# Rows of h by VectorE block turns and transfers over DRAM in place of TensorE transposes

## The chip, the cores and the metric

The kernel runs on one core of one Trainium2 chip. The metric is the device time of one execution in microseconds (us), taken as the median of several runs. The engines are TensorE (PE, its weight loads are listed as PEld), VectorE (DVE), ScalarE (ACT), GpSimd (POOL) and the queue engine SyncE (SP), which here only issues transfers.

## The reference

The inputs are x (16 batches x 1024 nodes x 128 features, fp32), one 1024 x 1024 matrix adj used by all batches, and small weights. Layer 0 is a graph convolution with a residual and a layer norm, layer 1 is a gated recurrent update that runs five steps on the same adj:

```python
x = layernorm(x + adj @ (x @ W0) + b0)
h = x
for _ in range(5):
    m  = adj @ h                                   # for every batch; used twice (m_in = m_out)
    av = concat([m, m])
    u3 = h @ u3_w.T + u3_b
    z  = sigmoid(av @ w3_w.T + w3_b + u3)
    r  = sigmoid(av @ w4_w.T + w4_b + u3)
    hv = tanh(av @ w5_w.T + w5_b + (r * h) @ u5_w.T + u5_b)
    h  = (1 - z) * h + z * hv
out = layernorm(x + h)
```

All arithmetic is fp32.

## The kernel before

**Tiling.** The batches go through in four quads of four (`QUAD`). `adj` is transposed once and kept in SBUF. The product adj times four batches, `aggregate` (L340), is done with a two-level Strassen-like scheme: seven outer products instead of eight, each again seven inner ones. It runs as four chains of matmuls (`chain`, L296) named by their outer products: chain 12 (products 1 and 2), chain 3, chain 67 and chain 54. A chain runs its inner products in a fixed order, 1, 5, 6, 2, 7, 3, 4, with hooks: work that is hung in front of an inner product. In a chain the stationary operand of a matmul is a 128 x 128 block of h (or of sums of blocks), the moving operand 256 columns of adj or of its sums. One fp32 matmul is two matmul instructions of the profile. Chains 12, 67 and 54 have 28 matmuls each, chain 3 has 14.

**Two layouts of h.** `rows` holds h with nodes on the partitions: `rows[p, k, c, d]` is node 8p + c of batch k, feature d, so that `rows[:, k, c, :]` is a stationary block for chunk c. `hid` holds h with features on the partitions, for the gates. DVE forms the outer sums of blocks into `tsum` (`outer_sums`, L286) and the inner ones into `inner` (`sums_of`, L282, `inner_sums`, L265).

**A recurrent step.** The program loops over quads q and steps s (L536). After `aggregate` has left m in `agg` (features on the partitions), for each batch k `gate_half` (L396) runs three matmuls per half of the nodes, and `update` (L420) two, a tanh on ACT and three operations on DVE that leave the new h in `hid` (L430 to L432). The next step's aggregation needs the new h in `rows`: `back_to_rows` (L441) transposes each of the eight chunks of a batch on PE into PSUM (`turn`, L434, L438), and ACT copies them to `rows` (L444), 512 columns at a time. In steps 1 to 4 batches 0 and 1 are turned between the gates, batches 2 and 3 in hooks 6 and 7 of chain 12. Then come the sums: the inner sums of batches 0 and 1 (L267 to L270) are wanted by product 5 of chain 12, the rows and sums of batches 2 and 3 by chain 3, the outer sums (L290 to L294) by chains 67 and 54. In step 0 of a quad it is the other way round: `rows` comes from DRAM and `to_hidden` (L446) makes `hid` by transposes, hung into chains 3 and 67.

**Order.** The tile framework orders the instructions of each engine by priority and by its own estimate of times, and puts in the semaphores; after that each engine runs its list in order. Transfers of the recurrent part are issued by SP. PSUM banks for gates and transposes come from a pool of three (`bank`, L88).

Of the kernel before, what the change touches and what calls it, by code (L numbers as in the profile page):

```python
# [20 lines left out]
def kernel(  # L21
# [29 lines left out]

    nc = tc.nc
# [4 lines left out]
    QT = N // 4  # L57
    CH = C // 2
# [11 lines left out]
    rows = const.tile([P, QUAD, C, D], F32, name="rows")  # L70
    hid = const.tile([P, QUAD, N], F32, name="hid")
    agg = const.tile([P, QUAD, N], F32, name="agg")
    tsum = const.tile([P, 4, 2, CH, D], F32, name="tsum")
    first = const.tile([P, 2, N], F32, name="first")
    hvs = const.tile([P, 2, HALF], F32, name="hvs")
    inner = [const.tile([P, 4, 2, 2, D], F32, name=f"inner{i}") for i in range(2)]
    ypad = [const.tile([P, C, D], F32, name=f"ypad{i}") for i in range(2)]

    z_of = [tsum[:, i].rearrange("p k c d -> p (k c d)") for i in (1, 0)]
    rh_of = [tsum[:, i].rearrange("p k c d -> p (k c d)") for i in (2, 3)]  # L80
    hid_rows = hid.rearrange("p b (c d) -> p b c d", c=C)
    saved = dram.tile([B, P, N], F32, name="saved")

# [9 lines left out]

    def load(q, dst, src_of, ks=range(QUAD)):
        for k in ks:
            nc.sync.dma_start(dst[:, k], src_of(q * QUAD + k))

    def x_rows(b):
        return as_rows(b, x)

    def saved_rows(b):
        return saved[b].rearrange("p (c d) -> p c d", c=C)
# [3 lines left out]
    adj_rows = adj.rearrange("(p c) m -> c p m", c=C)  # L106
    raws = [agg[:, c] if c < CH else hid[:, c - CH] for c in range(C)]
    for h in range(2):
        for c in range(h * CH, h * CH + CH):
            queues[c % 2].dma_start(raws[c], adj_rows[c])  # L110
        for k in (2 * h, 2 * h + 1):
            queues[k % 2].dma_start(rows[:, k], x_rows(k))
# [159 lines left out]
    def blocks_of(src, ns):  # L272

        halves = src.rearrange("p b (h j c) d -> p b h j c d", h=2, j=2)
        if ns == (1, 2):
            return lambda j, k: halves[:, k, :, j]
        if ns == (3,):
            return lambda j, k: halves[:, 2 + k, 1:2, j]
        at = {(6, 7): slice(1, 3), (5, 4): slice(0, 4, 3)}[ns]
        return lambda j, k: tsum[:, at, k, 2 * j : 2 * j + 2]  # L280

    def sums_of(src, ns):  # L282
        t = inner[0 if ns in ((1, 2), (6, 7)) else 1]
        inner_sums(blocks_of(src, ns), [t[:, i, : len(ns)] for i in range(4)])

    def outer_sums(src, early=True, late=True):  # L286

        lo, hi = src[:, 0:2], src[:, 2:4]
        if early:
            nc.vector.tensor_sub(tsum[:, 2], hi[:, :, CH:], hi[:, :, :CH])  # L290
            nc.vector.tensor_add(tsum[:, 1], tsum[:, 2], lo[:, :, :CH])
        if late:
            nc.vector.tensor_sub(tsum[:, 0], hi[:, :, :CH], lo[:, :, :CH])
            nc.vector.tensor_sub(tsum[:, 3], lo[:, :, CH:], tsum[:, 1])  # L294

    def chain(tag, src, ns, results, hooks, order=(1, 5, 6, 2, 7, 3, 4)):  # L296


        xs = blocks_of(src, ns)
        t = inner[0 if ns in ((1, 2), (6, 7)) else 1]  # L300
        w = len(ns) * QT
        right = {
            1: xs(0, 0), 2: xs(1, 0), 3: xs(1, 1), 4: t[:, 3], 5: t[:, 0], 6: t[:, 1], 7: t[:, 2],
        }
# [19 lines left out]
        for a in order:  # L324
            for hook in hooks.get(a, ()):
                hook()
            for o, n in enumerate(ns):
                for c in range(2):
                    nc.tensor.matmul(  # L329
                        bank_of[a][:, ts(o, QT)], right[a][:, o, c, :], left[n][a][:, c, :],  # L330
# [9 lines left out]
    def aggregate(tag, src, hooks):  # L340

        c12 = agg[:, 2:4, :HALF]
        room = src.rearrange("p b c d -> p b (c d)")
# [5 lines left out]
        def into(t):  # L349
# [3 lines left out]
        chain(f"12_{tag}", src, (1, 2), into(first), hooks.get(12, {}))  # L353
        sums_of(src, (6, 7))
        nc.vector.tensor_add(agg[:, 0:2, :HALF], two(first[:, 0]), two(first[:, 1]))
        chain(
            f"3_{tag}", src, (3,), lambda i, k: agg[:, 2 + k : 3 + k, ts(i, QT)], hooks.get(3, {}),
        )
        sums_of(src, (5, 4))
        p6, p7, p5, p4 = (room[:, k] for k in range(4))  # L360
        chain(f"67_{tag}", src, (6, 7), into(room[:, 0:2]), hooks.get(67, {}))
# [4 lines left out]
            f"54_{tag}", src, (5, 4), into(room[:, 2:4]), hooks.get(54, {}),  # L366
# [9 lines left out]
    def project(q, k, y):  # L376

        b = q * QUAD + k
        for h in range(2):
# [6 lines left out]
            for c in range(CH):  # L386
                nc.tensor.matmul(  # L387
                    po3[:, c, :], agg[:, k, ts(h * CH + c, P)], w0_sb, start=False, stop=True,
                    skip_group_check=True,
                )  # L390
            with tc.high_priority():
                nc.vector.tensor_add(y[:, ts(h, CH), :], po3, y[:, ts(h, CH), :])
        layernorm(y, f"0_{b}", saved_rows(b))
# [26 lines left out]
    def update(tag, k):  # L420

        z, rh = z_of[k % 2], rh_of[k % 2]
        for h in range(2):
# [8 lines left out]
            nc.vector.tensor_add(hid[:, k, cols], hid[:, k, cols], hv)  # L432

    def turn(name, src):  # L434
        pt = bank(name)
        pt3 = pt.rearrange("p (k q) -> p k q", k=CH)
        for c in range(CH):
            nc.tensor.transpose(pt3[:, c, :], src(c), ident)  # L438
        return pt3

    def back_to_rows(tag, k):  # L441
        for h in range(2):
            pt = turn(f"pt_{tag}_{k}_{h}", lambda c: hid[:, k, ts(h * CH + c, P)])
            nc.scalar.copy(rows[:, k, ts(h, CH), :], pt)  # L444

    def to_hidden(q, k):  # L446
        for h in range(2):
            pt = turn(f"pt0_{q}_{k}_{h}", lambda c: rows[:, k, h * CH + c, :])
            nc.scalar.copy(hid[:, k, ts(h, HALF)], pt.rearrange("p k q -> p (k q)"))

    def finish(q, k, y, now=False, parts=1):

        b = q * QUAD + k
        dst = as_rows(b, out)
        for h in range(2):
            cols = ts(h, CH)
            pt = turn(f"pt1_{b}_{h}", lambda c: hid[:, k, ts(h * CH + c, P)])
# [19 lines left out]
    rooms = [rows, hid_rows]  # L477
# [9 lines left out]
    for q in range(NQ):  # L487
        room = rooms[q % 2]
        hooks = {}
        if q == 0:  # L490
            hooks[12] = {
                5: [turn_rest],
                6: [outer_left, call(sums_of, rows, (3,))],
                7: [call(outer_sums, rows), call(inner_left, 6), call(inner_left, 7)],
# [3 lines left out]
            with tc.issue_after(last_left.ins):  # L498
                sums_of(rows, (1, 2))
        else:  # L500
            hooks[12] = projections(q - 1)
            hooks[12][6] = [call(sums_of, room, (3,)), call(outer_sums, room, False, True)]
# [12 lines left out]
        def ahead(room):  # L515
            sums_of(room, (1, 2))
            outer_sums(room, True, False)
# [5 lines left out]
        if q == 0:  # L523
            with tc.issue_after(last_left.ins):
                aggregate(f"x{q}", room, hooks)
        else:
            aggregate(f"x{q}", room, hooks)


    y_of = [ypad[0], ypad[1], hvs.rearrange("p h (c d) -> p (h c) d", c=CH), ypad[0]]  # L530
# [5 lines left out]
    for q in range(NQ):  # L536
        for s in range(STEPS):
            tag = f"{q}_{s}"
            if s == 0:
                hooks = {54: {}}  # L540
                if q == 0:
                    hooks[12] = projections(NQ - 1)
                    hooks[12][6] = [call(sums_of, rows, (3,)), call(outer_sums, rows, False, True)]
                else:
                    load(q, rows, saved_rows)
                    sums_of(rows, (1, 2))
                    sums_of(rows, (3,))
                    outer_sums(rows)
# [3 lines left out]
                hooks[3] = {6: [call(to_hidden, q, 0)], 7: [call(to_hidden, q, 1)]}  # L552
                hooks[67] = {
                    4: [call(to_hidden, q, 2)], "end": [call(drain, 99, 0), call(to_hidden, q, 3)],
                }
            else:
                def rest(tag=tag):
                    back_to_rows(tag, 3)
                    sums_of(rows, (3,))
                    outer_sums(rows)  # L560
                hooks = {12: {6: [call(back_to_rows, tag, 2)], 7: [rest]}, 54: {}}
            hooks[54][4] = [call(gate_half, tag, 0, 0)]
            aggregate(tag, rows, hooks)
            at = f"{q}_{s + 1}"
# [6 lines left out]
            update(tag, 0)  # L571
            gates(tag, 2)
            update(tag, 1)
# [4 lines left out]
            else:  # L578
# [46 lines left out]
```

## Time and profile before

| | |
|---|---|
| median of 4 runs | 1913.94 us (1912.38 to 1915.55) |
| the profiled execution's own time | 1913.82 us |
| its span, first to last instruction | 1911.9 us, mean granted TensorE clock 0.99 |
| busy: PE, DVE, ACT, POOL | 1868.8, 1190.1, 876.5, 95.1 us |
| transfers | 56.46 MB, 7.8% of 16 DMA engines' span on SP's and ACT's first queue |
| PE transposes of h (L438) | 768 instructions, 101.8 us busy |
| ACT copies of the transposed h (L444, L449) | 160 instructions, 86.0 us busy |

A profile gives, for one execution, every instruction with its start and length. A group line reads: line, engine, operation, out<-in by the program's names, shape, count | busy us, mean ns of one | idle time just before and who ended it. A line of a stage table reads: stage, its length, busy us and count of PE, PEld, DVE, ACT and POOL, the granted clock, the share of the DMA engines and their GB/s. Matmuls are pipelined: the length of one is longer than the distance between two that follow each other.

### The profile page before, as it was taken

The numbers are of one execution on the slowest core, as the hardware profiler recorded it, in microseconds if no ns is written. First come the engines' busy times: TensorE is split into PE (matmuls) and PEld (weight loads), VectorE is DVE, ScalarE is ACT, GpSimd is POOL, SyncE is SP. The second block draws the span as 40 slices with busy tenths as digits, with TensorE's granted clock in tenths as the row PEclk, the third lists the DMA queues.
The fourth block names the chain that finished last, engine by engine and source line by source line (L and its number), as shares of the span: only waits on it lengthen the run. The fifth ranks groups of instructions, "written<-read, shape, count | busy, mean of one in ns | idle before, by whom it ended". The sixth has DMA issues, their size and how long they took to land.

```text
span 1911.9 us, 20135 instructions
## 1 busy us (share of the span) xinstructions
PE 1868.8 (98%) x7421; PEld 1311.7 (69%) x7421; DVE 1190.1 (62%) x2172; ACT 876.5 (46%) x1582; POOL 95.1 (5%) x138
## 2 busy tenths in 40 slices
PE   8999999999999999999999999999999999999994
PEld 7888876675857667585675757667585766758662
DVE  7887846465565846556566755646558474655655
ACT  2445565435353553535444553543535544353544
POOL 0112110000000200000000100000000100000002
PEclk9999999999999999999999999999999999999997
DMA  5233310000001100000001200000001100000011
GB/s 212 67 128 121 106 67 0 1 1 1 1 0 45 55 34 0 1 1 0 1 0 45 88 1 1 1 1 1 1 11 56 44 1 0 1 0 0 1 44 44
DMA packets 16945, 56.46 MB, mean 30 GB/s; under 512 B 2512, under 2 KB 3408, under 8 KB 16848
## 3 DMA queue, kind: packets, MB, share of 16 engines
q1 hardware_dynamic: 15984, 52.05, 7.8%
q10 hardware_dynamic: 864, 3.15, 0.4%
q8 instruction: 58, 0.95, 0.2%
q14 instruction: 39, 0.32, 0.1%
HBM read 38.41 MB, written 16.78 MB: 29 GB/s over the span
## 4 chain that ended last, share of the span: by engine, by line
PE 89%; DVE 7%; ACT 2%; POOL 1%; issue 1%; DMA 0%; SPq 0%; ACTq 0%; POOLq 0%; DVEq 0%
PE pb L329 21%; PE pa L329 12%; PE pc L329 12%; PE pu L406 7%; PE pu L402 7%; PE seeded L411 7%; PE ph L426 7%; PE ph L427 7%; PE pt L438 4%; PE pc_x L329 2%; PE pa_x L329 2%; PE seeded L387 1%; DVE stats L227 1%; ACT ypad L237 1%; ACT rows L237 1%
## 5 line engine op out<-in xcount | busy, mean ns | idle before, releaser
L410 DVE TENSOR_TENSOR tsum<-tsum,hid 128x512 f32<-128x512 f32 x160 | 110.5, 691 | 182.4 <-ACT tsum L409 180.7
L329 PE MATMUL pb<-e,inner 128*128 128x256 f32 x864 | 207.5, 381 | 9.1 <-ACT pb L315 9.1
L329 PEld LDWEIGHTS pb<-e,inner 128*128 128x128 f32 x864 | 161.2, 190 | 31.5 <-ACT pb L315 11.0
L429 ACT ACTIVATE hvs<-ph,bh 128x512 f32<-128x512 f32 x160 | 109.9, 687 | 155.3 <-PE ph L427 138.6
L406 PE MATMUL pu<-agg,w_t 128*128 128x512 f32 x320 | 169.4, 611 | 0.0
L430 DVE TENSOR_TENSOR hvs<-hvs,hid 128x512 f32<-128x512 f32 x160 | 108.6, 687 | 95.7 <-ACT hvs L429 95.7
L426 PE MATMUL ph<-agg,w_t 128*128 128x512 f32 x320 | 165.2, 598 | 2.2 <-ACT hvs L429 2.2
L319 DVE TENSOR_TENSOR rows<-pb,rows 128x512 f32<-128x512 f32 x44 | 30.4, 691 | 217.1 <-PE pb L329 187.8
L427 PE MATMUL ph<-tsum,u_t 128*128 128x512 f32 x320 | 164.1, 595 | 0.0
L411 PE MATMUL seeded<-agg,w_t 128*128 128x512 f32 x320 | 163.4, 592 | 0.0
L402 PE MATMUL pu<-hid,u_t 128*128 128x512 f32 x320 | 156.8, 600 | 0.0
L329 PE MATMUL pb<-s,inner 128*128 128x256 f32 x576 | 153.4, 388 | 0.4 <-DVE agg L319 0.2
L409 ACT ACTIVATE tsum<-pu,br 128x512 f32<-128x512 f32 x160 | 110.0, 687 | 81.1 <-PE pu L406 81.0
L329 PE MATMUL pb<-a,inner 128*128 128x256 f32 x576 | 144.9, 380 | 0.2
L405 ACT COPY seeded<-pu 128x512 f32<-128x512 f32 x160 | 91.4, 571 | 116.7 <-PE pu L402 116.7
L329 PE MATMUL pc<-e,inner 128*128 128x256 f32 x560 | 134.1, 379 | 0.0
L329 PEld LDWEIGHTS pb<-s,inner 128*128 128x128 f32 x576 | 104.7, 190 | 39.1 <-DVE rows L319 17.5
L329 PEld LDWEIGHTS pb<-a,inner 128*128 128x128 f32 x576 | 108.9, 190 | 24.4 <-issue 9.6
L414 ACT ACTIVATE tsum<-seeded,bz 128x512 f32<-128x512 f32 x160 | 110.0, 687 | 27.3 <-PE seeded L411 27.3
L329 PEld LDWEIGHTS pc<-e,inner 128*128 128x128 f32 x560 | 106.1, 190 | 14.3
L432 DVE TENSOR_TENSOR hid<-hid,hvs 128x512 f32<-128x512 f32 x160 | 108.7, 688 | 8.4 <-PE pt L438 0.5
L427 PEld LDWEIGHTS ph<-tsum,u_t 128*128 128x128 f32 x320 | 60.9, 190 | 76.7 <-issue 72.4
(172 smaller groups left out, 2972.2 us busy)
## 6 DMA issues: line engine op xcount, KB each, us to landing
rows<-saved SPq DMA_DIRECT2D x20, 512.0 KB, 3.7
hid<-in_x_dram SPq DMA_DIRECT2D x12, 512.0 KB, 4.2
rows<-in_x_dram SPq DMA_DIRECT2D x10, 512.0 KB, 4.0
ypad<-saved SPq DMA_DIRECT2D x9, 512.0 KB, 3.3
out_dram<-ypad SPq DMA_DIRECT2D x9, 512.0 KB, 2.6
ypad<-in_x_dram SPq DMA_DIRECT2D x8, 512.0 KB, 3.6
saved<-ypad SPq DMA_DIRECT2D x8, 512.0 KB, 2.6
saved<-rows SPq DMA_DIRECT2D x4, 512.0 KB, 2.9
```

The costliest lines, as they stand in the source:

```text
L329: nc.tensor.matmul(bank_of[a][:, ts(o, QT)], right[a][:, o, c, :], left[n][a][:, c, :], start=(a in (1, 5) and o == 0 and c == 0), stop=(c ...
L402: nc.tensor.matmul(pu, w_t["u3"], hid[:, k, cols], start=True, stop=True, skip_group_check=True)
L406: nc.tensor.matmul(pu, w_t["w4"], agg[:, k, cols], start=False, stop=True, skip_group_check=True)
L409: nc.scalar.activation(rh[:, cols], pu, AF.Sigmoid, bias=br)
L410: nc.vector.tensor_mul(rh[:, cols], rh[:, cols], hid[:, k, cols])
L411: nc.tensor.matmul(pz, w_t["w3"], agg[:, k, cols], start=False, stop=True, skip_group_check=True)
L414: nc.scalar.activation(z[:, cols], pz, AF.Sigmoid, bias=bz)
L426: nc.tensor.matmul(ph, w_t["w5"], agg[:, k, cols], start=True, stop=False)
L427: nc.tensor.matmul(ph, w_t["u5"], rh[:, cols], start=False, stop=True)
L429: nc.scalar.activation(hv, ph, AF.Tanh, bias=bh)
L430: nc.vector.tensor_sub(hv, hv, hid[:, k, cols])
L432: nc.vector.tensor_add(hid[:, k, cols], hid[:, k, cols], hv)
```

## The change

`rows` of the recurrent steps is no longer made on PE and ACT. After each half of a batch's update (512 nodes) DVE turns the half in 32 x 32 blocks (`nc.vector.transpose`) into `ypad`, SP writes that to a DRAM tile `turned`, and reads it back in two transfers that put the blocks on the right partitions. Within a partition the result has the chunk c innermost: `rows[p, k, 8 d + c]`. A stationary block for one chunk is then every 8th word of a row; the inner sums keep two chunks side by side, the outer sums four, so their blocks are read at a step of 2 or 4 words. The flag `turned` selects this layout; layer 0 and step 0 of each quad, whose rows come from x or from the saved x, keep the old one. `to_hidden` is turned the other way with the same means, over half of `agg` and the same DRAM tiles, in other hooks (chain 3 products 5 and 2, chain 67 product 3 and its end), with the `drain` of waiting layer-norm work moved from the end of chain 67 to its product 3. `hid` and `agg` now have their columns in natural node order, so adj is loaded in plain blocks of 128 rows, and `project` and `finish` take every 8th column. The two turns of a batch come with `update` itself and no longer in hooks; the transposes of `finish` stay on PE.

The core of the diff (a few renamings of tiles to flat shapes are left out):

```diff
+    SQ = 32
+    A4 = P // SQ
...
+    turned = [
+        [dram.tile([P, HALF], F32, name=f"turned{i}_{h}") for h in range(2)] for i in range(2)
+    ]
...
+    def chunk_cols(t, c):
+        return t.rearrange("p (q c) -> p c q", c=C)[:, c]
...
-    adj_rows = adj.rearrange("(p c) m -> c p m", c=C)
...
-            queues[c % 2].dma_start(raws[c], adj_rows[c])
+            queues[c % 2].dma_start(raws[c], adj[ts(c, P)])
...
+    def blocks_of(src, ns, turned):
+        if ns in ((1, 2), (3,)):
+            if turned:
+                v = src.rearrange("p b (d h j c) -> p b h j d c", h=2, j=2, c=2)
+            else:
+                v = src.rearrange("p b (h j x) -> p b h j x", h=2, j=2)
...
+        if turned:
+            v = tsum.rearrange("p n b (d j c) -> p n b j d c", j=2, c=2)
...
+    def inner_of(ns, turned):
+        t = inner[0 if ns in ((1, 2), (6, 7)) else 1][:, :, : len(ns)]
+        if turned:
+            t = t.rearrange("p i o (d c) -> p i o d c", c=2)
+        return [t[:, i] for i in range(4)]
...
+    def outer_sums(src, turned=True, early=True, late=True):
+        t = [tsum[:, i] for i in range(4)]
+        if turned:
+            v = src.rearrange("p b (d h c) -> p h b d c", h=2, c=CH)
+            t = [x.rearrange("p b (d c) -> p b d c", c=CH) for x in t]
...
+        def chunk(a, o, c):
+            return right[a][:, o, :, c] if turned else right[a][:, o, ts(c, D)]
...
-                        bank_of[a][:, ts(o, QT)], right[a][:, o, c, :], left[n][a][:, c, :],
+                        bank_of[a][:, ts(o, QT)], chunk(a, o, c), left[n][a][:, c, :],
...
-                    po3[:, c, :], agg[:, k, ts(h * CH + c, P)], w0_sb, start=False, stop=True,
+                    po3[:, c, :], chunk_cols(agg[:, k], h * CH + c), w0_sb, start=False, stop=True,
...
-    def update(tag, k):
+    def update(tag, k, back=True):
...
             nc.vector.tensor_add(hid[:, k, cols], hid[:, k, cols], hv)
+            if back:
+                back_to_rows(k, h)
+
+    def back_to_rows(k, h):
+        cols = ts(h, HALF)
+        t = ypad[k % 2][:, cols]
+        nc.vector.transpose(
+            t.rearrange("p (b j c) -> p b c j", b=2, j=SQ),
+            hid[:, k, cols].rearrange("p (b i c) -> p b c i", b=2, i=SQ),
+        )
+        there = turned[k % 2][h]
+        nc.sync.dma_start(there, t)
+        src = there.rearrange("(a i) (b x) -> b i a x", a=A4, b=2)
+        for b in range(2):
+            nc.sync.dma_start(
+                rows[ts(2 * h + b, SQ), k].rearrange("p (a x) -> p a x", a=A4), src[b]
+            )
+
+    def to_hidden(k):
+        t = agg[:, ts(k % 2, 2), HALF:]
+        v = rows[:, k].rearrange("p (c a j) -> p c a j", c=C, a=A4)
+        for h in range(2):
+            nc.vector.transpose(
+                t[:, h].rearrange("p (a i c) -> p c a i", a=2, i=SQ), v[:, :, ts(h, 2)]
+            )
+            nc.sync.dma_start(turned[k % 2][h], t[:, h])
+            src = turned[k % 2][h].rearrange("(b j) (a x) -> a j b x", b=A4, a=2)
+            for a in range(2):
+                nc.sync.dma_start(
+                    hid[ts(2 * h + a, SQ), k].rearrange("p (b x) -> p b x", b=A4), src[a]
+                )
...
-    def back_to_rows(tag, k):
-        for h in range(2):
-            pt = turn(f"pt_{tag}_{k}_{h}", lambda c: hid[:, k, ts(h * CH + c, P)])
-            nc.scalar.copy(rows[:, k, ts(h, CH), :], pt)
-
-    def to_hidden(q, k):
-        for h in range(2):
-            pt = turn(f"pt0_{q}_{k}_{h}", lambda c: rows[:, k, h * CH + c, :])
-            nc.scalar.copy(hid[:, k, ts(h, HALF)], pt.rearrange("p k q -> p (k q)"))
...
-                hooks = {54: {}}
+                hooks = {
+                    3: {5: [call(to_hidden, 0)], 2: [call(to_hidden, 1)]},
+                    67: {3: [call(drain, 99, 0), call(to_hidden, 2)], "end": [call(to_hidden, 3)]},
+                    54: {},
+                }
...
-                hooks[3] = {6: [call(to_hidden, q, 0)], 7: [call(to_hidden, q, 1)]}
-                hooks[67] = {
-                    4: [call(to_hidden, q, 2)], "end": [call(drain, 99, 0), call(to_hidden, q, 3)],
-                }
...
-                def rest(tag=tag):
-                    back_to_rows(tag, 3)
-                    sums_of(rows, (3,))
-                    outer_sums(rows)
-                hooks = {12: {6: [call(back_to_rows, tag, 2)], 7: [rest]}, 54: {}}
+                hooks = {12: {7: [call(sums_of, rows, (3,)), call(outer_sums, rows)]}, 54: {}}
...
-            aggregate(tag, rows, hooks)
+            aggregate(tag, rows, hooks, s > 0)
...
-            update(tag, 0)
+            update(tag, 0, not last)
...
-            else:
-                back_to_rows(at, 0)
...
-            update(tag, 2)
+            update(tag, 2, not last)
             if not last:
-                back_to_rows(at, 1)
                 sums_of(rows, (1, 2))
```

## Prediction

> **What bounds the kernel now.** First the page's part 1: engines, busy time and share, instructions.
>
> ```profile
> PE 1868.8 (98%) x7421; PEld 1311.7 (69%) x7421; DVE 1190.1 (62%) x2172; ACT 876.5 (46%) x1582; POOL 95.1 (5%) x138
> ```
>
> TensorE (PE) is busy for 98%, the chain that ended last is PE for 89%. So I look for a stage where PE ever waits. The table by stages, for one middle recurrent step from the first product of its aggregation to that of the next:
>
> ```profile
> 892.62:973.93 81.31, 81.31 (x309) 55.30 (x308) 47.49 (x72) 35.55 (x60) 0.00 (x0) 1.00 0.00 1
> ```
>
> PE is busy for all 81.31 us (clock 1.00), VectorE (DVE) 47.5, ScalarE (ACT) 35.6, the transfers 0.00. Every us of work taken off PE here counts, until something else is late. Next the seam between two steps, in the timeline (start, length, then engine and line):
>
> ```profile
> 968.66 0.69 DVE L430 TENSOR_TENSOR hvs<-hvs,hid 128x512 f32<-128x512 f32 x1 [1.88 <-ACT hvs L429]
> ...
> 969.46 1.04 PE L438 MATMUL pt<-ident,hid 128*128 128x128 f32 x8
> ...
> 970.40 1.12 PE L426 MATMUL ph<-agg,w_t 128*128 128x512 f32 x2
> ...
> 972.12 0.69 DVE L267 TENSOR_TENSOR inner<-rows 128x512 f32<-128x512 f32 x1
> ...
> 973.93 1.89 PE L329 MATMUL pa<-a,rows 128*128 128x256 f32 x8
> ...
> 975.66 1.89 PE L329 MATMUL pc<-e,inner 128*128 128x256 f32 x8
> ...
> 977.39 1.04 PE L438 MATMUL pt<-ident,hid 128*128 128x128 f32 x8
> ...
> 978.26 1.89 PE L329 MATMUL pb<-e,inner 128*128 128x256 f32 x8
> ...
> 983.02 1.23 DVE L293 TENSOR_TENSOR tsum<-rows 128x1024 f32<-128x1024 f32 x1 [4.20 <-ACT rows L444]
> ```
>
> A batch's eight transposes hold PE for 970.40 - 969.46 = 0.94 us (0.87 at 977.39). Eight passes of 256 columns take 975.66 - 973.93 = 1.73, that is 0.216 a pass; an fp32 product is two passes, 0.43. The inner sums (L267) are ready 2.9 us before PE asks for them. Batch 3's rows come from ACT at 983, three products before they are needed. Last the groups, by shape, and the transfers (KB, median us to landing):
>
> ```profile
> L430 DVE TENSOR_TENSOR hvs<-hvs,hid 128x512 f32<-128x512 f32 x160 | 108.6, 687 | 95.7 <-ACT hvs L429 95.7
> L227 DVE BATCH_NORM_STATS2 stats<-ypad 128x6 f32<-128x128 f32 x136 | 34.0, 266 | 0.0
> L163 PE MATMUL pt_adj<-ident,hid 128*128 128x128 f32 x32 | 4.0, 283 | 0.0
> L163 PEld LDWEIGHTS pt_adj<-ident,hid 128*128 128x128 f32 x32 | 4.0, 193 | 0.1
> L438 PEld LDWEIGHTS pt<-ident,rows 128*128 128x128 f32 x128 | 14.8, 140 | 1.8 <-ACT hid L449 0.4
> ```
>
> ```profile
> hvs<-saved SPq DMA_DIRECT2D x3, 512.0 KB, 3.1
> ...
> out_dram<-rows SPq DMA_DIRECT2D x2, 256.0 KB, 2.0
> ...
> hvs<-in_L_gnn_u_w_dram SPq DMA_DIRECT2D x2, 64.0 KB, 2.1
> ```
>
> **Taken away.** 16 recurrent steps (s = 1 to 4 in four quads) turn four batches: 2 x 0.94 + 2 x 0.87 = 3.62 us of PE each, 58 us in all. The four s = 0 steps lose to_hidden's transposes: 4 x 0.87 = 3.5 us each, 14 us. The 160 ACT copies (594 ns each) go too; PE waits for none of them in this stage, so I cost them at nothing.
>
> **Strided weights** (every 2nd, 4th or 8th word, in the 16 turned aggregations, project and finish). L163 loads weights at a step of 8 words: 193 ns instead of 140, but 32 of them pass in 4.0 us, 0.125 each, at the pace of the ACT copies behind them. The next load starts when the product before it does and has 0.216 us, so I take nothing. The other end is below (strided load rival). **Strided sums**: the turned sums on DVE read runs of 2 or 4 words with gaps. No row shows such an operation; ends: as now, and 1.75 times as long; I take no change: the nearest rows are the present sums of the same sizes (0.42, 0.69, 1.22 us), and no row gives a reason to leave them.
>
> **The turn itself** (L472, 128 x 512 on DVE, single words 32 bytes apart on both sides). DVE's 512-element operations follow each other every 0.60 us when independent, 0.73 when one needs the other (L430 to L431). Ends: 0.60, and 1.38 (two passes of 0.69, filling and emptying a block). I take 1.06 us: L227, the slowest row per element on DVE, needs 266 ns for 128, four times that for 512. [...]
>
> **The round trip.** SP issues per half batch one write of 256 KB and two reads of 128 KB, in order: write h0, write h1, the reads of h0, the reads of h1, each waiting for its write. Write: 2.0 us (the 256 KB row). Read: between 2.1 (64 KB) and 3.1 (512 KB); I take 2.4. Issues are 0.4 us apart, hand-overs 0.1. SP has nothing else to do in the middle steps; its loads and stores at the quad ends now stand in one queue with the turns.
>
> **The path at the seam**, t = 0 where the next aggregation starts. DVE's work on batch 2 begins at 973.93 - 968.66 - 0.94 = 4.33 us before that. The order of the changed kernel's instructions puts on DVE, ahead of the inner sums (now L278): eight update operations (2 x 0.73 + 6 x 0.60 = 5.06) and two turns (2.12). L278 starts at 2.85, ends at 3.5. Batch 1's rows are there by then (its last turn ends some 6 us before t = 0, and the way takes 0.1 + 2.0 + 0.1 + 0.4 + 2.4 = 5.0). PE asks for L278 after product 1 and one gate product that the order puts there: 1.73 + 0.86 = 2.6. **First wait: 1.0.** Behind L278 on DVE stand its three siblings, batch 3's update and two turns: 5.2 + 2.12, the last turn ends at 10.2. Rows of batch 3 land 5.0 later, 15.2. PE reaches chain 3 after 28 x 0.43 + 0.86 + 1.0 = 14.0. **Second wait: 1.2.** From then DVE has 4 x 0.33 + 4 x 1.13 + 0.6 = 6.4 us to the first sum of chain 67, PE 10 us of work (14 x 0.43, three gate products that the order moves there, 1.73): covered. After a wait PE loses another 0.13 or so (in the timeline two passes start at 911.63, the next, released by DVE, at 912.21, 0.15 later than their 0.43): 0.26. Balance per step: -3.62 + 1.0 + 1.2 + 0.26 = -1.16; times 16 = -18.6 us.
>
> **The s = 0 steps.** The eight turns (8.5 us of DVE) fall into chains 3 and 67; those of batches 2 and 3 reuse half of agg and so wait for a write to land (2.0) while the additions of chain 67 (L350), for which PE waits, stand behind them. drain(99, 0) moves earlier. Ends per quad: 0 and 8.5 + 2 x 2.0 = 12.5. DVE is busy for 53.7 of 81.3 us in such a step, so most is hidden: I take 4.0, four quads 16, against the 14 saved: +2.
>
> **Sum**: 1913.8 (the profiled execution's own time, span 1911.9; the median of the four is 1913.94) - 18.6 + 2 = **1897 us**, -0.9%.
>
> **Rivals.**
> *Turn at full rate* (0.60): L278 starts at 1.93, no first wait; the last turn ends at 8.3, rows at 13.3 against 13.0, 0.3 of wait. Balance -3.2, 16 steps -51, s = 0 hidden further, -5: 1858. For it: all 512-element operations here cost the same. Against: none of them hops.
> *Tail too long* (turn 1.38, read 3.1): L278 ends at 4.2, wait 1.6; last turn 11.5, rows at 17.2 against 14.6, wait 2.6. Balance +0.84, 16 steps +13, s = 0 +4: 1931, slower. For it: DVE works without a pause from -4.3 to 11.5. With the other terms as taken it decides from a turn of some 1.35 us (each us of turn costs 4 us a step).
> *Strided sums slow* (the other side by one mechanism): place, the turned sums; at 1.75 times, L278's three siblings delay batch 3's turns by 1.8, and the path from its rows to chain 67 grows from 6.4 to 11.2 plus 0.7 of additions, 1.7 over PE's 10: +3.5 a step, 1953. It decides from about 1.25 times.
> *Strided loads slow*: 53 ns more on L329's 190 is 243, 27 over the 216 of a pass; 16 x 98 x 2 = 3136 loads, +85: 1982. It decides from some 222 ns. Against: the 0.125 us of L163.
> *The gain does not arrive*: waits equal to the 3.6 taken away, 1914; the balance lies only 1.2 us from it.
>
> **How the numbers follow.** A difference under 0.2% (3.8 us) can't be told from none. As costed 0.42 (1878 to 1914 with the turn between 0.9 and 1.35), full rate 0.13, tail too long 0.23, strided sums 0.10, strided loads 0.05, queue or s = 0 stalls worse than taken 0.07. Faster: 0.34 + 0.13 = 0.47; same: 0.08 of the first and 0.03 of the third, 0.11; slower 0.42. The range must reach both ways: 1860 leaves out part of the full-rate case, 1962 the strided loads and the worst of the sums. The likeliest case alone: 1878 to 1914.
>
> **What would show it.** Right: a middle step of about 80.1 us; PE without pt rows, waiting about 1 us at pc<-e,inner of chain 12 for DVE and about 1.2 at the first product of chain 3 for the transfer; turns near 1.1 us; L329 still 0.216 a pass; sums still 0.69 and 1.22. Wrong: LDWEIGHTS spaced beyond 0.216, sums longer than 0.7, a transfer of rows over 3 us, or PE waiting in s = 0 steps for more than 4 us.

## The result, and the profile after

The changed kernel takes 1916.8 us (median, 1913.4 to 1922.5), the kernel before 1913.0 in the same comparison: a ratio of **1.0022, 95% interval [1.0016, 1.0027]**. It is slower by 0.2%, where 0.9% faster was forecast. The profiled execution took 1914.9 us, its span is 1913.1.

The kernel has 640 matmul instructions less on TensorE, and yet takes no less time. First the engines (part 1 of the page, after the change; before, PE was busy for 1868.8 us with 7421 instructions):

```profile
PE 1851.9 (97%) x6781; PEld 1352.2 (71%) x6781; DVE 1340.6 (70%) x2332; ACT 793.4 (41%) x1422; POOL 94.5 (5%) x138
```

The transposes are gone, but PE is busy only 17 us less, and its weight loads (PEld) take 40 us more. So some of the instructions that stayed became longer. To see where, I cut both executions at the first product of every turned aggregation and add up the stages. The two stage tables, before and then after (stage, length, busy us and count of PE, PEld, DVE, ACT, POOL, clock, share of the DMA engines, GB/s):

```profile
0.00:315.67 315.67, 304.27 (x1457) 246.99 (x1458) 235.10 (x551) 153.69 (x317) 47.02 (x70) 0.99 0.31 106
559.62:640.09 80.47, 80.46 (x301) 54.44 (x300) 52.96 (x95) 33.63 (x56) 3.10 (x4) 1.00 0.08 27
640.09:729.99 89.90, 87.68 (x350) 60.59 (x349) 54.45 (x120) 49.77 (x96) 9.33 (x12) 0.98 0.13 47
```

```profile
0.00:337.93 337.93, 329.38 (x1410) 273.03 (x1411) 246.70 (x560) 146.92 (x305) 48.67 (x70) 0.99 0.35 114
578.91:660.56 81.65, 80.48 (x285) 57.48 (x284) 59.75 (x104) 31.41 (x52) 2.63 (x4) 1.00 0.24 78
660.56:745.48 84.92, 81.79 (x301) 55.61 (x300) 62.21 (x126) 43.80 (x84) 9.06 (x12) 0.98 0.30 99
906.13:986.45 80.32, 79.23 (x277) 56.63 (x276) 55.00 (x79) 31.41 (x52) 0.00 (x0) 1.00 0.16 53
```

The forecast of each stage follows from the prediction's terms (per seam -3.62 + 1.0 + 1.2 + 0.26, with half of the transposes on either side of it; -3.5 + 4.0 for to_hidden):

| stage | before | after | change | forecast |
|---|---|---|---|---|
| layer 0 and step 0 of the first quad | 315.67 | 337.93 | +22.3 | -1.3 |
| 12 middle steps | 975.8 | 963.9 | -11.9 | -13.9 |
| 3 last steps of a quad | 241.4 | 245.0 | +3.5 | +2.0 |
| 3 first steps of a quad | 267.1 | 253.9 | -13.2 | -3.9 |
| last step and end | 112.0 | 112.4 | +0.4 | +0.6 |

The middle steps came out nearly as forecast (80.32 us for 80.15; below it turns out that two errors of opposite sign meet there), the first steps better. The forecast fell in the first row. Nearly all of it is layer 0: the first recurrent aggregation starts at 244.75 us for 224.22. Layer 0 contains no turn at all; of the changed lines it runs `project`, with every 8th column as weights, for three of the four quads (the fourth falls into step 0). The groups of project's products and loads, before:

```profile
L387 PE MATMUL seeded<-w_sb,agg 128*128 128x128 f32 x256 | 33.9, 288 | 1.8 <-ACT seeded L384 1.7
L387 PEld LDWEIGHTS seeded<-w_sb,agg 128*128 128x128 f32 x256 | 31.3, 199 | 6.8 <-ACT seeded L384 6.6
```

and after, with those of the chains by the distance of the words that they load (rows: 8 words, tsum: 4, inner: 2), the transposes of `finish` (8 words) and the turn:

```profile
L419 PE MATMUL seeded<-w_sb,agg 128*128 128x128 f32 x256 | 64.0, 403 | 0.0
L419 PEld LDWEIGHTS seeded<-w_sb,agg 128*128 128x128 f32 x256 | 62.3, 334 | 3.4 <-ACT seeded L416 3.2
L360 PEld LDWEIGHTS pa<-a,rows 128*128 128x128 f32 x320 | 76.8, 304 | 8.7 <-PE ph L458 3.8 <-DMA turned<-agg 0.7 <-issue 0.7
L360 PEld LDWEIGHTS pa<-s,tsum 128*128 128x128 f32 x320 | 76.7, 297 | 3.0
L360 PEld LDWEIGHTS pb<-e,inner 128*128 128x128 f32 x864 | 168.4, 196 | 33.1 <-ACT pb L346 14.8
L503 PEld LDWEIGHTS pt<-ident,hid 128*128 128x128 f32 x128 | 17.8, 194 | 10.0 <-issue 8.4 <-ACT hvs L461 1.1
L472 DVE STREAM_TRANSPOSE ypad<-hid 128x512 f32<-128x512 f32 x128 | 144.3, 1128 | 0.5
```

Project's 256 passes take 64.0 us for 33.9: **30 us**. In the chains a load from rows or tsum takes about 300 ns as a mean over all steps, the ones not turned (190) included; from inner 196. In the timeline of the seam the eight passes over rows take 908.02 - 906.13 = 1.89 us, those over inner 913.38 - 911.66 = 1.72. Summed over a middle step from start to start, the 84 passes over rows and tsum went from 18.29 to 19.88 us, from 0.218 to 0.237 each: 1.59 a step, **25 us** over 16. So the passes whose loads take words 4 or 8 apart follow each other every 0.237 us with 256 columns (chains) and every 0.240 with 128 (project). Against the 0.218 and the 0.123 from start to start in the kernel before, that is 0.02 more and about twice as much. That the loads are the reason is tested in e1 to e3.

The seam itself, in the timeline of the changed kernel (start, length, engine, line, what; in brackets the wait before it and who ended it):

```profile
906.13 2.05 PE L360 MATMUL pa<-a,rows 128*128 128x256 f32 x8
908.02 1.02 PE L434 MATMUL pu<-hid,u_t 128*128 128x512 f32 x2
908.04 1.11 DVE L472 STREAM_TRANSPOSE ypad<-hid 128x512 f32<-128x512 f32 x1
909.07 0.64 DVE L278 TENSOR_TENSOR inner<-rows 128x512 f32<-128x512 f32 x1
909.85 1.97 PE L360 MATMUL pc<-e,inner 128*128 128x256 f32 x8 [0.80 <-DVE inner L278]
911.66 1.89 PE L360 MATMUL pb<-e,inner 128*128 128x256 f32 x8
913.38 2.08 PE L360 MATMUL pa<-a,rows 128*128 128x256 f32 x8
...
915.26 1.14 DVE L472 STREAM_TRANSPOSE ypad<-hid 128x512 f32<-128x512 f32 x1
...
920.66 1.12 PE L360 MATMUL pa<-s,rows 128*128 128x256 f32 x4
921.48 1.23 DVE L385 TENSOR_TENSOR agg<-first 128x1024 f32<-128x1024 f32 x1 [1.65 <-ACT first L352]
922.62 0.42 DVE L278 TENSOR_TENSOR inner<-rows 128x256 f32<-128x256 f32 x1
...
928.97 0.42 DVE L351 TENSOR_TENSOR agg<-pc,agg 128x256 f32<-128x256 f32 x1 [2.65 <-PE pc L360]
929.31 1.22 DVE L323 TENSOR_TENSOR tsum<-rows 128x1024 f32<-128x1024 f32 x1
...
932.74 1.97 PE L360 MATMUL pc<-e,inner 128*128 128x256 f32 x8 [0.29 <-DVE inner L278]
```

The first wait is where it was forecast (0.80 for 1.0). At 920.66, the first product of chain 3, PE does not wait at all. A third line, not forecast, is a wait of 0.29 us at chain 67: VectorE stood idle for 2.65 us at L351, an addition that waits for PE, with L323 and the wanted inner sums behind it.

### The profile page after: what moved, and what is told of

Its sections match the earlier page's. It is cut to its first block, busy times and chain, and to the rows that moved or that the text cites. A ratio compares the mean times of both kernels' runs of the same rounds, so it can differ in the third digit from the quotient of the medians.

```text
span 1913.1 us, 19986 instructions
## 1 busy us (share of the span) xinstructions
PE 1851.9 (97%) x6781; PEld 1352.2 (71%) x6781; DVE 1340.6 (70%) x2332; ACT 793.4 (41%) x1422; POOL 94.5 (5%) x138
## 4 chain that ended last, share of the span: by engine, by line
PE 79%; DVE 15%; issue 2%; ACT 2%; DMA 1%; POOL 0%; DVEq 0%; SPq 0%; ACTq 0%; POOLq 0%
PE pb L360 21%; PE pc L360 13%; PE pa L360 10%; PE pu L438 7%; PE seeded L443 7%; PE pu L434 6%; PE ph L459 4%; PE ph L458 4%; PE seeded L419 3%; PE pc_x L360 2%; PE pa_x L360 2%; DVE hvs L462 2%; DVE ypad L472 2%; DVE hvs L463 2%; DVE tsum L323 1%
## 5 line engine op out<-in xcount | busy, mean ns | idle before, releaser
L360 PEld LDWEIGHTS pb<-e,inner 128*128 128x128 f32 x864 | 168.4, 196 | 33.1 <-ACT pb L346 14.8
L360 PE MATMUL pc<-e,inner 128*128 128x256 f32 x560 | 136.7, 384 | 17.5 <-DVE inner L278 17.5
L472 DVE STREAM_TRANSPOSE ypad<-hid 128x512 f32<-128x512 f32 x128 | 144.3, 1128 | 0.5
L360 PEld LDWEIGHTS pb<-s,inner 128*128 128x128 f32 x576 | 110.7, 198 | 21.3 <-DVE rows L350 7.8
L458 PEld LDWEIGHTS ph<-agg,w_t 128*128 128x128 f32 x320 | 60.7, 190 | 79.1 <-issue 75.1
```

The lines of the kernel that those rows point to most:

```text
L360: nc.tensor.matmul(bank_of[a][:, ts(o, QT)], chunk(a, o, c), left[n][a][:, c, :], start=(a in (1, 5) and o == 0 and c == 0), stop=(c == 1) ...
L458: nc.tensor.matmul(ph, w_t["w5"], agg[:, k, cols], start=True, stop=False)
L472: nc.vector.transpose(t.rearrange("p (b j c) -> p b c j", b=2, j=SQ), hid[:, k, cols].rearrange("p (b i c) -> p b c i", b=2, i=SQ),)
```

## The experiments

Two theories for the missing time. **S**: loads of words that lie apart are slower than the products over them; the 55 us are theirs. **Order**: the waits of the seam come from the order in which VectorE, PE and SP run their lists, not from the length of the turn or of the way over DRAM. The rivals are that the loads were hidden after all, and that the round trip itself is too long.

**e1: project loads adjacent words.**

```diff
-                    po3[:, c, :], chunk_cols(agg[:, k], h * CH + c), w0_sb, start=False, stop=True,
+                    po3[:, c, :], agg[:, k, ts(h * CH + c, P)], w0_sb, start=False, stop=True,
```

> The changed kernel, but project loads 128 adjacent words of agg as weights in place of every 8th word (the columns that it takes are then not those of its chunk: this leaves the right order of the nodes out, no work). Theory S (a load of single words some way apart takes longer than a product lasts): the 256 passes of project go from 0.240 us back to the 0.1225 of the kernel before, 30 us less than the changed kernel: 1884 to 1890. Rival H (the loads are hidden, as predicted, and project is longer because of what it waits for): no change, 1914 to 1919.

Measured: 1892.7 us, ratio to before 0.9891 [0.9869, 0.9913], by the two ratios some 25 us less than the changed kernel. The groups of project in e1:

```profile
L419 PE MATMUL seeded<-w_sb,agg 128*128 128x128 f32 x256 | 33.0, 283 | 1.8 <-ACT seeded L416 1.7
L419 PEld LDWEIGHTS seeded<-w_sb,agg 128*128 128x128 f32 x256 | 30.5, 194 | 6.7 <-ACT seeded L416 6.5
```

The passes are back at their old length, and the first turned aggregation starts 27.1 us earlier (310.83 for 337.93). H has fallen. The time is 3 us above S's range, and the gain 5 us short of the 30: the three first steps of the later quads became 6.4 us longer (260.3 for 253.9). PE waits longer there for ScalarE's copies into pb (15.4 us in the whole execution for 12.0), which is half of it. The rest, and why, was not tested.

**e2: the chains load adjacent words.** `turned = False` at the head of `chain` for the weights, the sums left as they are.

```diff
     def chain(tag, src, turned, ns, results, hooks, order=(1, 5, 6, 2, 7, 3, 4)):
+        turned = False
         xs = blocks_of(src, ns, turned)
```

> The changed kernel, but the products of the turned aggregations load 128 adjacent words as weights; the sums on VectorE keep the chunk-innermost layout (so weights and sums don't belong together: the right chunks are left out, no work). Theory S: the 84 passes per step over rows and tsum (every 8th and 4th word) go from 0.237 to 0.216, 1.6 us a step, 25 us over 16 steps, of which the waits for VectorE may take back up to a third: 1891 to 1900. Those over inner (every 2nd word) were at 0.216 already and stay. Rival H: no change, 1914 to 1919.

Measured: 1897.7 us, 0.9917 [0.9895, 0.9940]. The loads are short again; one group for the others:

```profile
L361 PEld LDWEIGHTS pa<-s,tsum 128*128 128x128 f32 x320 | 60.8, 190 | 8.3
```

A middle step takes 79.02 us for 80.32: of the 1.59 us a step 0.3 went into longer waits for the inner sums (22.3 us in all for 17.5, up to 1.0 each). S holds for the chains too.

**e3: the price of a load by its distance**, in the kernel before, batch by batch in project.

```diff
+    def pick(b, t, c):
+        s = b // 2 + 1
+        return t[:, : s * P].rearrange("p (n s) -> p s n", s=s)[:, c % s]
...
-                    po3[:, c, :], agg[:, k, ts(h * CH + c, P)], w0_sb, start=False, stop=True,
+                    po3[:, c, :], pick(b, agg[:, k], h * CH + c), w0_sb, start=False, stop=True,
```

> The kernel before, but project loads every s-th word of agg, s = 1 for batches 0 and 1, 2 for batches 2 and 3, and so on to 8 for batches 14 and 15 (wrong columns, the same work). It prices the load by its step. Theory S with a threshold: 0.12 us a pass at steps 1 and 2, about 0.24 from step 4 on, step 3 open; the whole some 19 to 24 us over the kernel before, 1932 to 1938. A price that grows evenly with the step would show 0.14 at 2, 0.17 at 4, 0.24 at 8, about 1927. Rival H: 0.12 throughout, 1913.

Measured: 1935.7 us in one run. The timeline, 16 passes for each batch; the batches with s = 1, 2, 3, 3, 4 and 4 (the second batch with s = 2 ran at a clock of 0.58 and is left out):

```profile
67.53 2.05 PE L391 MATMUL seeded<-w_sb,agg 128*128 128x128 f32 x16
...
79.42 2.15 PE L391 MATMUL seeded<-w_sb,agg 128*128 128x128 f32 x16
...
126.85 3.05 PE L391 MATMUL seeded<-w_sb,agg 128*128 128x128 f32 x16
133.29 3.06 PE L391 MATMUL seeded<-w_sb,agg 128*128 128x128 f32 x16
140.50 3.79 PE L391 MATMUL seeded<-w_sb,agg 128*128 128x128 f32 x16
148.27 3.94 PE L391 MATMUL seeded<-w_sb,agg 128*128 128x128 f32 x16
```

Against the 2.05 us at s = 1, a distance of 2 costs next to nothing (2.15), 3 half as much again (3.05 and 3.06), 4 nearly twice (3.79 and 3.94); from there it is flat (3.63 to 4.08 us up to s = 8). The median load is 192 ns at s = 1, 196 at 2, 261 at 3 and 316 to 335 from 4 on. The price in this run is a staircase, not a line.

**e4: to_hidden by PE again**, back_to_rows as changed.

```diff
-            nc.vector.transpose(
-                t[:, h].rearrange("p (a i c) -> p c a i", a=2, i=SQ), v[:, :, ts(h, 2)]
-            )
...
+            for c in range(CH):
+                nc.tensor.transpose(pt3[:, c, :], rows[:, k, ts(h * CH + c, D)], ident)
+            to = hid[:, k].rearrange("p (q c) -> p q c", c=C)[:, :, ts(h, CH)]
+            nc.scalar.copy(to, pt.rearrange("p (c q) -> p q c", c=CH))
```

> The changed kernel with one part undone: to_hidden by TensorE transposes and ScalarE copies again (into the chunk-innermost hid), back_to_rows as changed. Theory C (in the s = 0 steps the eight turns and their ways over DRAM cost PE next to nothing, against the 4.0 us a quad of the prediction): PE gets 3.5 us a quad back to do, 14 in all, little else changes: 1926 to 1934. Rival P (the prediction's term was right: 16 us of stalls against 14 of transposes): 1912 to 1918.

Measured: 1924.3 us, 1.0068 [1.0051, 1.0085], by the two ratios about 9 us over the changed kernel. Of the 14 us of transposes that come back, 9 are seen, so the turns there cost about 1.3 us a quad and not 4.0. C was nearer, though its range began 2 us too high.

**e5: the four inner sums ahead of batch 3's update**, in the changed kernel; order alone.

```diff
-                sums_of(rows, (1, 2))
+                ready = sums_of(rows, (1, 2))
...
-                update(tag, 3, not last)
+                with tc.issue_after(ready.ins):
+                    update(tag, 3)
```

> The changed kernel, with batch 3's update on VectorE put behind the four inner sums of batches 0 and 1 (order only; it computes the reference). In the changed kernel PE waits 0.80 us for the first of these sums in each of 16 steps and loses 0.17 more to the refill. Theory D (that wait is VectorE's order alone): the first sum starts some 1.2 us earlier, the wait goes, batch 3's last turn ends when it did: 0.95 us a step, 15 in all, 1898 to 1905. Rival T (batch 3's rows have no slack: its first half now goes to DRAM later, and the sums over batches 2 and 3 wait for it): the wait moves there, 1910 to 1920.

Measured: 1900.4 us, 0.9945 [0.9930, 0.9960]; a middle step 79.45. PE's waits for the sums in the whole execution (us, times, longest), in the changed kernel and then in e5:

```profile
PE pc L360 <- DVE inner L278: 17.5, 32, 0.8
PE pc L360 <- DVE inner L278: 4.6, 16, 0.3
```

The wait of 0.8 is gone in all 16 seams, the 0.29 at chain 67 is left. Batch 3's rows had room: its last turn ends 10.3 us after the seam, as before, and no wait took the place.

**e6: also the two outer sums that only chain 54 needs behind chain 3.**

```diff
-                hooks = {12: {7: [call(sums_of, rows, (3,)), call(outer_sums, rows)]}, 54: {}}
+                hooks = {12: {7: [call(sums_of, rows, (3,)), call(outer_sums, rows, True, True, False)]}, 54: {}}
+                hooks[3] = {'end': [call(outer_sums, rows, True, False, True)]}
```

> As e5, and the two outer sums that only the last chain needs (tsum 0 and 3) stand behind chain 3 in the program, and so on VectorE behind the inner sums for chain 67; it computes the reference. In e5 PE still waits 0.29 us a step there, and loses 0.17 to the refill. Theory D (that wait is VectorE's order: the two sums, 1.14 us each, and an addition that waits for PE stand ahead): it goes, 0.4 a step, 7 in all: 1890 to 1896. Rival T (it comes from the rows of batch 3 over DRAM): 1898 to 1903.

Measured: 1894.0 us, 0.9905 [0.9889, 0.9922]; a middle step 78.90. No wait of PE for VectorE's sums is left in the turned steps. Both waits of the seam were order.

**g1: a layout without far words.** If S is right, a layout that never loads further apart than every 2nd word gets the 55 us back. Columns of hid and agg are ordered (pair of chunks, node, chunk of the pair), rows (pair, feature, chunk of the pair). A half batch then goes back in four reads with runs of 256 bytes. (`adj` is loaded in two pieces for each block of 128 rows; that part of the edit is left out here.)

```diff
-        return t.rearrange("p (q c) -> p c q", c=C)[:, c]
+        return t.rearrange("p (k q c) -> p k c q", k=CH, c=2)[:, c // 2, c % 2]
...
-            return right[a][:, o, :, c] if turned else right[a][:, o, ts(c, D)]
+            if turned:
+                return right[a][:, o].rearrange("p (d c) -> p c d", c=2)[:, c]
+            return right[a][:, o, ts(c, D)]
...
+    def bounce(k, h, t, dst):
+        there = turned[k % 2][h]
+        nc.sync.dma_start(there.rearrange("j p x -> p j x"), t.rearrange("p (j x) -> p j x", j=2))
+        src = there.rearrange("j (a i) (b x) -> b i (j a) x", a=A4, b=A4)
+        for b in range(A4):
+            nc.sync.dma_start(
+                dst[ts(b, SQ), k, ts(h, HALF)].rearrange("p (y x) -> p y x", y=2 * A4), src[b]
+            )
```

> The changed kernel with another layout, which computes the reference: chunks lie in pairs, so that no weights are further apart than every 2nd word; the sums on VectorE read and write adjacent words; a turn hops by 2 words in place of 8. For that a half batch's way over DRAM is one write in runs of 1 KB and four reads in runs of 256 bytes, in place of one write and two reads in runs of 1 KB. Theory S: the 30 us of project and the 25 us of the chains come back, 1916.8 - 55 = 1862 (1855 to 1868). Rival T (the way over DRAM is what counts now): four reads issued 0.4 apart and four times the packets bring batch 3's rows 1 to 3 us later, PE waits that much in each of 16 steps: 1878 to 1910. Rival H: 1914 or more.

Measured: 1921.1 us, 1.0043 [1.0025, 1.0062]. Two groups of g1 (a load from rows, the turn) and its largest wait on PE:

```profile
L352 PEld LDWEIGHTS pc<-e,rows 128*128 128x128 f32 x240 | 47.4, 197 | 5.2
L464 DVE STREAM_TRANSPOSE ypad<-hid 128x512 f32<-128x512 f32 x128 | 90.5, 707 | 0.5
```

```profile
PE pu L430 <- DVE agg L377: 31.0, 16, 1.9
```

The time lies in H's range, but the rows contradict H: the loads are fast (197 ns) and the first turned aggregation starts at 314.11, 24 us earlier. What took it back is the turned steps: a middle step mostly takes 81.52 us (82.0 as a mean of the twelve), 1.2 more than in the changed kernel. The framework has put the work in another order: the second product of chain 12 that reads rows starts 2.6 us after the seam, for 7.3 in the changed kernel. Why it did so is not shown.

**g2 and g3: order in g1.** g2 puts two gate products behind chain 3's first two products; g3 in addition puts batch 3's update behind the first inner sum. Of g2's edit, the first of the two products:

```diff
+        with tc.issue_after(behind.ins) if behind else nullcontext():
             nc.tensor.matmul(
                 pu, w_t["w4"], agg[:, k, cols], start=False, stop=True, skip_group_check=True
             )
...
-            hooks[54][4] = [call(gate_half, tag, 0, 0)]
+            hooks[54][4] = [lambda tag=tag: gate_half(tag, 0, 0, product[2, 1])]
```

> The kernel with steps of 2 words (g1), with two gate products of batch 0 (over agg) put behind the first two products of chain 3 in PE's order; it computes the reference. In g1 these products stand right behind chain 12 and PE waits 1.94 us a step there for ScalarE's copy and VectorE's addition of agg. Theory O (g1's loss is the order of the instructions): 1.5 to 2 us a step less, 24 to 32 in all: 1889 to 1898. Rival T (g1's loss is the longer way over DRAM): batch 3's rows come no earlier, the wait moves to the sums over batches 2 and 3: 1908 to 1922.

> As g2, and batch 3's update on VectorE stands behind the first of the inner sums of batches 0 and 1 as well. Theory O: the other wait of g1 (0.57 us a step for that sum, and 0.1 of refill) goes too, 10 us less than g2: 1879 to 1888. Rival T: the turns of batch 3 end some 1.8 us later by it, its rows come too late for the sums over batches 2 and 3, and PE loses 0.5 to 1.5 us a step there: 1890 to 1910.

Measured: g2 1899.6 us, 0.9942 [0.9925, 0.9958], 2 us above O's range, a step of 80.79: the wait of 1.9 went, and a new one of 1.3 came in chain 3, for an addition of VectorE (20.3 us in all). g3 1948.4 us, 1.0194 [1.0179, 1.0209], above both ranges: PE now waits for the first inner sum, up to 3.9 us, and that sum waits for rows from DRAM (111.9 us in 31 places). Behind it VectorE's whole update of batch 3 is late. So rows of batch 1 come late in g3, which is T's mechanism at an earlier place, but not yet why they do.

**g4: whole batches over DRAM**, in g2: one write and four reads a batch, with the orders of e5 and e6. In short:

```diff
+        nc.sync.dma_start(there.rearrange("k p x -> p k x"), t.rearrange("p (k x) -> p k x", k=CH))
+        src = there.rearrange("k (a i) (b x) -> b i (k a) x", a=A4, b=A4)
+        for b in range(A4):
+            nc.sync.dma_start(dst[ts(b, SQ), k].rearrange("p (y x) -> p y x", y=CH * A4), src[b])
```

> g2 with three changes; it computes the reference. A batch goes over DRAM as a whole (one write of 512 KB and four reads of 128 KB, where g2 has two writes and eight reads), batch 3's update stands behind the four sums as in e5, and the late outer sums behind chain 3's additions. Theory: rows of batch 3 land some 7 us after its last turn in place of 8 or more, PE waits under 0.9 us a step in place of 2.9: step of 78.0 to 78.9 us, with layer 0 as in g2, 1850 to 1870. Rival T (the way over DRAM still ends too late, for the first sums from batch 1 or for those over batches 2 and 3): 1.5 us a step and more stay, 1875 to 1905.

Measured: 1951.4 us, 1.0204 [1.0188, 1.0219], above both ranges, with steps of 83 to 84 us. This time the trace names the cause. The queue of SP at one seam (L478 writes, L484 reads), and then the sum that waits on VectorE:

```profile
895.69 8.62 SPq L478 DMA_DIRECT2D turned<-ypad  x2
904.42 4.89 SPq L484 DMA_DIRECT2D rows<-turned  x8
```

```profile
910.24 0.69 DVE L280 TENSOR_TENSOR inner<-rows 128x512 f32<-128x512 f32 x1 [6.33 <-DMA rows<-turned]
```

The two writes are those of batch 1, at 895.69, and of batch 2, which has to wait for batch 2's turn. Only behind it come the reads of batch 1, eight in a row with those of batch 2. Batch 1 had been in DRAM since about 898.6 (the writes of g4 land after 2.9 us, the median). SP's list, not the transfer, held it for some 6 us. The queues of g2 and g3 show the same pattern, though in g2 VectorE hardly waits for these rows (0.2 us in all).

**g5: one constraint more**, SP's write of a batch behind the reads of the batch before.

```diff
+        with tc.issue_after(done["read"].ins) if "read" in done else nullcontext():
             nc.sync.dma_start(there...
...
-            nc.sync.dma_start(
+            done["read"] = nc.sync.dma_start(
```

> g4, and on SP's queue the write of a batch stands behind the four reads of the batch before it; nothing else is moved, and it computes the reference. In g4 SP has the write of batch 2 ahead of the reads of batch 1: issued at 895.69 and, when batch 2 is turned, about 904, then the reads at 904.42, and VectorE's first sum waits 6.33 us for them. Theory Q (g4's loss, and part of g1's to g3's, is SP's order): the sum no longer waits, the step goes from 84.2 to 78.5 to 79.5 us: 1856 to 1876. Rival W (a way of 2.9 + 3.2 us is too long by itself): over 1.5 us a step stay, 1890 to 1940.

Measured: 1873.9 us, 0.9798 [0.9783, 0.9812]; a middle step 78.48. One constraint on SP's order took 5.3 us off a middle step (83.8 in g4 as a mean of the twelve). VectorE's waits for the rows, in g4 and then in g5:

```profile
DVE inner L280 <- DMA rows<-turned: 146.4, 32, 6.8
DVE inner L280 <- DMA rows<-turned: 0.9, 2, 0.5
```

Q holds, W has fallen.

**g6: the remaining waits of g5 by order.**

```diff
+            early = turned and a == 2 and len(ns) == 1
+            behind = done["start"] if early else None
+            if turned and ns == (1, 2) and a != order[0]:
+                behind = product[order[order.index(a) - 1], 2]
+            with tc.issue_after(behind.ins) if behind else nullcontext():
                 for o, n in enumerate(ns):
...
+            with tc.issue_after(done[7, 1].ins):
+                nc.vector.tensor_sub(dst[3], xs(1, 0), dst[1])
```

> g5 with the waits that are left by its order taken out by order alone: the products of chain 12 in their old order, one gate product of hid between the first two of chain 3 (the second writes the bank that ScalarE still copies: 0.50 us a step), and the fourth inner sum for chain 67 behind chain 3's additions (which PE waits for: 1.4 us a step at most in g4). It computes the reference. Theory O (TensorE's work is then the bound again: 81.31 - 3.62 us of transposes, and little else): a step of 77.7 to 78.3 us, 1826 to 1845. Rival D (VectorE's queue is too full at the seam, a wait moves and does not go): a step of 78.7 to 79.5, 1850 to 1872.

Measured: **1865.7 us, 0.9761 [0.9742, 0.9781]**. The middle step is as theory O has it; the whole is 20 us over O's range (and falls in D's). Most of that stands in PE's waits outside the middle steps:

```profile
PE pu L449 <- DVE agg L404: 12.9, 8, 1.7
PE pt_adj L174 <- DMA agg<-in_adj_dram: 3.3, 1, 3.3
```

The first is new in g5 and g6: twice in each first step of a quad a gate product waits for the addition L404, which stands behind other work in VectorE's list; the first steps of the later quads take 87.3 to 87.7 us for 83.8 to 85.2 in the changed kernel. The second is the loading of `adj` at the start. Why the framework orders the first steps so is open. A middle step of g6 (columns as in the stage tables):

```profile
873.42:951.05 77.63, 77.48 (x278) 53.15 (x276) 52.25 (x79) 31.47 (x52) 0.00 (x0) 1.00 0.20 55
```

81.31 - 77.63 = 3.68 us: the whole of the transposes, with PE busy from end to end again, although transfers and VectorE do more than in the middle step of before (a DMA share of 0.20 for 0.00, 52.25 us for 47.49).

## Why the prediction was wrong, step by step

- **PE is the bound, and the transposes are worth 3.62 us a seam**: right. g6 gets 3.68.
- **"Strided weights ... I take nothing"**: this is the step that failed. The term was put at nothing; the passes show 55 us, of which e1 and e2 get 25 and 20 back. It had two faults. The row taken as the nearest, L163 (193 ns, 0.125 apart), is the load of a transposition. `finish` shows the same kind after the change, 194 ns at 8 words; a product's load at 8 words takes 334. The kinds are not alike. And the sentence that a load "has 0.216 us" holds for products of 256 columns. Project, named in the same line, has 128 columns and had 0.12. The prediction's own other end, 243 ns a load, was nearly the pace of a pass (0.237 to 0.240 measured). But it was counted on all 3136 loads of the chains (85 us), of which only 84 in 196 lie more than 2 words apart (25 us), and not on project's 256 (30 us).
- **Strided sums at nothing**: right. Inner sums over tsum took 682 ns (680 before), the outer ones 1.22 us. The other end, 1.75 times as long, was a supposition; no run shows it.
- **A turn of 1.06 us**: right in size (1.03 from start to start, 908.04 to 909.07), but by luck: it was four times a row of another operation on adjacent words, L227. No row of before has VectorE turn a block. Nor is 1.03 a price for every such turn: in g1 too single words hop, by 2 words in place of 8, and a turn takes 0.63 from start to start, 1.2 ns a column for 2.0 here. The upper end, 1.38 for filling and emptying a block in two passes, was a supposition; the turns are 1.13 us long, and 0.71 in g1.
- **Round trip**: write 2.0 as taken, read 2.5 for 2.4.
- **First wait 1.0**: right (0.80, and 0.17 lost behind the wait; L278 starts 2.94 after the aggregation, 2.85 was forecast). e5 shows that it is VectorE's order and can be had for nothing.
- **Second wait 1.2 at chain 3**: wrong. The last turn ended at 10.2 after the seam as forecast, but chain 3's first two products read batch 2 alone; batch 3 is first needed by L278 at 922.62, 16.5 after the seam. That stands in the program (`blocks_of` gives batch 2 for k = 0) and was read wrongly. In its place came 0.29, and the loss behind it, at chain 67, called covered by a sum of durations that left out that VectorE would stand at L351. VectorE ran its list in order there: it stood for 2.65 us, and L323, the next, began at 929.31, behind L351.
- **Waits together**: 2.46 a seam were taken; -0.99 + 3.62 - 1.59 = 1.04 were found. The 1.42 too much, 23 us in all, nearly hide the 25 us of the strided loads in the chains: that a middle step came out at 80.32 for 80.15 is luck.
- **Step 0: 4.0 us of stalls a quad**: too much. The row read for it (53.7 of 81.3 us busy) is that of a last step of a quad; a first step had 54.45 of 89.90, so more room. The first steps of the later quads gained 4.4 us each of the 5.3 that their transposes (3.5 + 1.81) were worth, and e4 gives 1.3 us of stalls.
- **The sum**: -58 - 14 of transposes, +30 of project, +25 of the chains, +17 of waits (16 x 1.04), +4 in the first steps, -2 at the start, where the first 32 transposes of adj take 5.6 us for 7.7 from start to start, waits for loading included: +2; the two profiled executions differ by 1.1. The gain was there, and a cost of the same size, nearly all of it strided loads and queue order, took it. Against the forecast the loads alone are 55 us; the miss is only some 18 because waits and stalls had been put some 35 us too high.

## What to carry to other kernels

A layout is paid for by everyone who reads it: before taking a stationary operand at a distance, list every product that loads it, with its number of columns, and compare the load with that product's own time (here loads of some 335 ns, in project and from rows, against passes that came every 0.12 us in project and every 0.22 in the chains). Price a load from a row of the same kind: at 8 words a transpose's load took 194 ns, project's 334. And look at the order in every queue at a seam, the one that only issues transfers included: in g4 what waited at its head held batch 1 for some 6 us, where a write took 2.9 and a read 3.2. After a change of layout look at the order on every engine again: in g1 the framework changed it (a product 2.6 us after the seam for 7.3).

## What was not expected of the hardware

- The weight loads of project's fp32 products went up a staircase by distance in e3: 192, 196, 261, then 316 to 335 ns for 1, 2, 3 and 4 to 8 words. Loads for transposes at 8 words took 194 ns (L503 after the change).
- VectorE's block turn of 128 x 512 took 1.13 us with words 8 apart and 0.71 with words 2 apart (g1), about as much as an addition of that size (0.69).
- ScalarE's copy of 128 x 512 that reads every 128th word of PSUM and writes runs of 4 words (e4) took 587 ns, no more than the 594 of the copies to adjacent words before.
